# Layer 0's aggregate ahead of the last row block of layer 3's first product, its attention read with a stride

## The chip, the core and the metric

The kernel runs on one NeuronCore of a Trainium2 chip. The metric is the device time of one execution, in microseconds (us), of that core. All data are float32. The engines go by the profile's names: PE is TensorE's matmuls and PEld its weight loads, DVE is VectorE, ACT is ScalarE, POOL is GpSimd, SP is the queue that issues most plain DMAs.

## The reference, cut to what matters

Four graph layers follow each other on `x` of 128 samples x 128 nodes x 256 features, each with a residual and a layer norm. Layer 0 is an edge attention; the other three mix nodes with matrices made of `adj` and multiply by weights.

```python
# layer 0: 512 edges (src, dst), 4 heads of 64 features
Xq = (H @ W_lin.T).reshape(bt, n, h, dh);  Xv = (H @ W_val.T).reshape(bt, n, h, dh)
e = einsum('behd,hd->beh', leaky_relu(Xq[:, src] + Xq[:, dst], 0.2), a) + log(A0[src, dst] + 1e-8)
attn = segment_softmax(e, src)                     # over the edges of one source node
Y = segment_sum(attn[..., None] * Xv[:, dst], src) # the aggregate
x = layernorm(x + Y.reshape(bt, n, d) @ W_out.T)
# layer 1: x = layernorm(x + three products with adj * adj between them)
# layer 2: x = layernorm(x + three products with split adj)
# layer 3: h = relu(batchnorm((A_hat @ x) @ W1.T)); x = layernorm(x + batchnorm(h @ W2.T))
```

Layer 3's batch norms need statistics over all samples, so the kernel has two phases: the first runs layers 0 to 2 and layer 3's first product, the second the rest of layer 3.

## The kernel before

The first phase works on 32 quads of four samples. `iteration(k)` runs one step of a software pipeline over five quads at once: `a = k-1` is in layers 2 and 3, `c = k` in the second and third products of layer 1, `b = k+1` gets its layer 0 aggregate and the start of layer 1, `e = k+2` its attention weights and `g = k+3` its query and value products and the gather of its edges. The order of every engine's instructions is the order in which the code is written: each engine executes its own instructions in that order, and semaphores hold an instruction until what it reads is there.

The attention weights of a quad go through memory. `scatter` writes them by an indirect DMA (on POOL's queue) into a dense matrix `attd` in DRAM, at row target x 128 + source, with R = 16 numbers in a row, one for each of the 4 samples x 4 heads. A DMA on SP's queue then loads the matrix as the tile `ad`: 128 partitions (targets), and on each 128 sources x 16 numbers. So the 128 attention weights of one sample and head lie 16 floats, that is 64 bytes, apart.

`by_row` copies `ad` into `adc`, in which these 128 weights lie beside each other. A call handles one sample (4 heads, 512 floats on each partition), and four calls make a quad. In `iteration` they are lambdas placed between the products of `second`, after products 1, 3, 8 and 10, and run on ACT. In `iteration_0` they stand around `third(0, 2)`, in `start` ACT and DVE take two each.

`stage_a` uses `adc`. For each sample and each half of the features it issues two matmuls, one for each head: the values `xv` (128 targets x 64 features) are the weights, and the head's 128 attention columns are the moving operand. `tile_position=(0, h * DH)` puts the two heads into the two column halves of the array. Each program matmul of float32 stands in the profile as two weight loads and two matmuls, so a quad's 16 are 32 in the trace (tile `py`). ACT copies each half of the result from PSUM to `yt`, 16 matmuls (tile `po`) multiply it by `wo`, and DVE adds the result to `xr` and normalizes.

In `iteration` the order on PE around this is: `second(c)`, `stage_f(a)` (tile `pa`), `values(g, i)` (tile `pq`), the four row blocks `hidden(a, 0..3)` of layer 3's first product (tile `ph` of line 552), `stage_a(b)` (lines 288 and 297), the transposes of `attention(e)` (tile `pat`), and `third(c)` (tile `p` of line 462). ACT copies each row block to `z` (line 555), then makes the two `yt` copies (line 291). The softmax of quad `e` is advanced a step after each `values` and each `hidden`. SP's and POOL's queues carry the load of `ad`, the store of `z` and the gathers in the order of `values`, `hidden`, `gather`, `scatter`. PSUM tiles come from a ring of 8 banks, `xt`, `yt`, `mx` and the like from a ring of 6.

Of the kernel before, what the change touches and what calls it, by code (L numbers as in the profile page):

```python
# [8 lines left out]
F32 = mybir.dt.float32  # L9
# [15 lines left out]
def gnn_stack(ctx: ExitStack, tc: tile.TileContext, x, adj, w_qv_t, a, w_out_t, src, dst,  # L25
# [14 lines left out]
    nc = tc.nc  # L40
    B, N, D = x.shape
    H, DH = a.shape
    E = src.shape[0]
    P = 128
# [3 lines left out]
    QB = 4  # L48
    NQ = B // QB
    R = QB * H  # L50
# [3 lines left out]
    K3 = F3 // P  # L54
# [8 lines left out]
    def ps(name):  # L63
        return psum.tile([P, 512], F32, tag="ps", name=name)
# [21 lines left out]
    def batch_norm(stats, c, vecs, scale, shift, slot):  # L86

        b, gamma, beta = (vecs[:, i, c:c + 1] for i in range(3))
        t = bn_t[:, slot]
        nc.vector.bn_aggr(t[:, 0:2], stats[:, c].rearrange("p q s -> p (q s)"))  # L90
        nc.scalar.activation(t[:, 2:3], t[:, 1:2], AF.Sqrt, bias=eps)
        nc.vector.tensor_scalar(t[:, 3:4], t[:, 0:1], b, b, op0=ALU.add, op1=ALU.subtract)
        nc.vector.reciprocal(t[:, 2:3], t[:, 2:3])
        nc.vector.tensor_mul(scale[:, c:c + 1], gamma, t[:, 2:3])
        nc.vector.scalar_tensor_tensor(shift[:, c:c + 1], t[:, 3:4], scale[:, c:c + 1], beta,
                                       op0=ALU.mult, op1=ALU.subtract, reverse1=True)
# [25 lines left out]
    def layer_norm(pool, r):  # L122
        mv = norm_stats(pool, r)
        norm_apply(pool, r, mv, norm_root(pool, mv))


    with ExitStack() as phase:
# [5 lines left out]
        quads = [Quad() for _ in range(NQ)]  # L133
# [7 lines left out]
        wk = phase.enter_context(tc.tile_pool(name="wk", bufs=2))  # L141
# [24 lines left out]
        def temp(name):  # L166
            return wk.tile([P, 512], F32, tag="t", name=name, bufs=6)
# [98 lines left out]
            s.ad = wk.tile([P, N * R], F32, tag="ad", name=f"ad{k}", bufs=1)  # L266
            nc.sync.dma_start(s.ad, ad[:N * N, :].rearrange("(t s) r -> t (s r)", s=N))

        def by_row(k, j, copy=None):

            s = quads[k]
            if j == 0:
                s.adc = wk.tile([P, R, N], F32, tag="adc", name=f"adc{k}", bufs=1)
            (copy or nc.scalar.copy)(s.adc[:, j * H:(j + 1) * H, :],
                                     s.ad.rearrange("p (s r) -> p r s", r=R)[:, j * H:(j + 1) * H, :])

        def stage_a(k):

            s = quads[k]
            yts = []  # L280
            for j in range(0, QB, 2):
                py = ps("py").rearrange("p (b c n) -> p b c n", b=2, c=DC)
                for t in range(2):
                    for dc in range(DC):
                        for h in range(2):
                            r0 = (j + t) * H + dc * 2 + h
                            d0 = dc * P + h * DH
                            nc.tensor.matmul(py[h * DH:(h + 1) * DH, t, dc, :], s.xv[:, j + t, d0:d0 + DH], s.adc[:, r0, :],
                                             start=True, stop=True, tile_position=(0, h * DH))
                yt = temp("yt").rearrange("p (b c n) -> p b c n", b=2, c=DC)  # L290
                nc.scalar.copy(yt, py)
                yts.append(yt)
            for j in range(0, QB, 2):
                po = ps("po").rearrange("p (b d) -> p b d", d=D)
                for t in range(2):
                    for dc in range(DC):
                        nc.tensor.matmul(po[:, t, :], yts[j // 2][:, t, dc, :], wo[:, dc, :],
                                         start=(dc == 0), stop=(dc == DC - 1))
                xj = s.xr[:, j:j + 2, :]
                nc.vector.tensor_add(xj, xj, po)  # L300
                layer_norm(wk, xj)
# [244 lines left out]
        def hidden(k, c):  # L546
            s = quads[k]
            if c == 0:
                s.zt = zpool.tile([P, K3, QB * N], F32, tag="z", name="z", bufs=1)
            ph = ps("ph3")  # L550
            for dc in range(DC):
                nc.tensor.matmul(ph, l3w1[:, dc, c * P:(c + 1) * P], s.ag[dc],  # L552
                                 start=(dc == 0), stop=(dc == DC - 1))
            if k < NQ - 1:
                nc.scalar.copy(s.zt[:, c, :], ph)
            nc.vector.bn_stats(st1[:, c, k, :], ph)
            if k == NQ - 1:
                kept["z"] = s.zt
                batch_norm(st1, c, bn1, sc1, sh1, c)
                nc.scalar.activation(s.zt[:, c, :], ph, AF.Relu, bias=sh1[:, c:c + 1], scale=sc1[:, c:c + 1])  # L560
            elif c == K3 - 1:
                nc.sync.dma_start(z_dram[k], s.zt.rearrange("p c n -> p (c n)"))
# [21 lines left out]
        def iteration(k):  # L584
            a, c, b, e, g = k - 1, k, k + 1, k + 2, k + 3
            has_c, has_b, has_e, has_g = c < NQ, b < NQ, e < NQ, g < NQ
            if has_b and b > 2:
                quads[b].xr = load_x(b)
            if a > 0:
                stage_e(a, c if has_c else None)  # L590
            elif has_c:
                late_sums(c)
            if has_c:
                between = {i: [] for i in range(14)}
                if has_e:
                    for c_, i in enumerate((0, 2, 7)):
                        between[i].append(lambda c_=c_: score(e, c_))
                if has_b:
                    for j, i in enumerate((1, 3, 8, 10)):
                        between[i].append(lambda j=j: by_row(b, j))  # L600
                if has_g:
                    between[11].append(lambda: values_in(g, quads[g].xg))
                second(c, between)
                if has_e:
                    score(e, NE - 1)
            if has_g and g + 1 < NQ:
                quads[g + 1].xg = load_x(g + 1, "xg", 1, ws)
            stage_f(a)
            steps = softmax_parts(e) if has_e else iter(())
            for i in range(QB):  # L610
                if has_g:
                    values(g, i)
                if i > 1:
                    next(steps, None)
            for i in range(K3):
                hidden(a, i)
                next(steps, None)
            if has_g:
                gather(g)
            if has_b:  # L620
                stage_a(b)
            if has_e:
                attention(e)
                scatter(e)
            if has_c:
                third(c, 0)
                if has_b:
                    third(c, 2)
                    third_mix(c, 0)
                    mix1(b, 0)  # L630
                    third_norm(c, 0)
                else:
                    third(c, 2, lambda: third_mix(c, 0))
                    third_norm(c, 0)
                third_mix(c, 2)
            if has_b:
                mix1(b, 2)
                first(b, 0)
            if has_c:
                third_norm(c, 2)  # L640
            if has_b:
                firsts(b)
# [7 lines left out]
        def iteration_0():  # L650

            late_sums(0)
            between = {i: [] for i in range(14)}
            between[1] = [lambda: attention(1), lambda: scatter(1)]
            for c, i in enumerate((2, 5, 7)):
                between[i].append(lambda c=c: score(2, c))
            second(0, between)
            score(2, NE - 1)
            gather(3)
            third(0, 0)  # L660
            steps = softmax_parts(2)
            next(steps)
            for j in (0, 1):
                by_row(1, j)
            third(0, 2)
            next(steps)
            for j in (2, 3):
                by_row(1, j)
            third_mix(0, 0)
            third_norm(0, 0)  # L670
            third_mix(0, 2)
            third_norm(0, 2)
            stage_a(1)
            for _ in steps:
                pass
            attention(2)
            scatter(2)
            stage_e(0)
            mix1(1, 0)
            mix1(1, 2)  # L680
            first(1, 0)
            firsts(1)

        def start():
# [164 lines left out]
            gather(2)  # L849
            for c in range(NE - 1):  # L850
                score(1, c)
            for j in range(QB):
                by_row(0, j, nc.vector.tensor_copy if j % 2 else None)
            stage_a(0)
            for i in range(QB):
                values(3, i, nc.scalar.copy)
# [23 lines left out]
    with ExitStack() as phase:  # L880
        bufs = phase.enter_context(tc.tile_pool(name="bufs", bufs=1))
        cst = phase.enter_context(tc.tile_pool(name="cst3", bufs=1))
        keep = phase.enter_context(tc.tile_pool(name="keep", bufs=1))
        wk = phase.enter_context(tc.tile_pool(name="wk3", bufs=2))
# [294 lines left out]
```

## Time and profile before

| what | value |
|---|---|
| time, median of 3 runs | 3283.32 us (3282.48 to 3291.94) |
| the profiled execution's own time | 3313.41 us |
| its span, first to last instruction | 3311.7 us |
| mean granted TensorE clock in it | 0.991 |
| PE / PEld busy | 3204.4 us (97%) / 2388.9 us (72%) |
| DVE / ACT / POOL busy | 1923.6 us (58%) / 1188.8 us (36%) / 656.6 us (20%) |
| `py` matmuls, line 288 | 1024, in 32 groups of 32 |
| `adc` copies, line 274 | 126 on ACT, 2 on DVE |

All durations below come from the profiled execution, which took 0.9% longer than the median. A line "engine line out<-in ... xcount" of the timeline merges instructions of one form that follow each other; the number in brackets is the engine's idle time before it and what ended it. Matmuls overlap in the array, so the duration of one in a table (273 ns for a `py`) is longer than the time between the starts of two.

### The profile page before, as it was taken

The page shows a single profiled execution, that of the slowest core. Times are in us where ns is not written, and L with a number is a line of the kernel's source. Part 1 is how long each engine was busy: PE and PEld are TensorE (multiplying, and loading weights), DVE is VectorE, ACT ScalarE, POOL GpSimd, SP SyncE. Part 2 cuts the span into 40 slices and gives each one's busy share as a digit, 9 for nine tenths or more (in the row PEclk, how much of TensorE's full clock was granted, in tenths as well). Part 3 has the DMA queues.
Part 4 walks back from the last instruction along what each step waited for, and adds up shares of the span by engine and source line. Part 5 has one row for each costly group of instructions (what it writes and reads, how often), then busy time and mean ns, then how long its engine had stood idle before and what let it go on. Part 6 is the DMA issues. An engine that isn't in the chain of part 4 may idle for free. (4 is left out here: it accounts for less than half of the span.)

```text
span 3311.7 us, 38376 instructions
## 1 busy us (share of the span) xinstructions
PE 3204.4 (97%) x14804; PEld 2388.9 (72%) x14804; DVE 1923.6 (58%) x3702; ACT 1188.8 (36%) x2104; POOL 656.6 (20%) x541
## 2 busy tenths in 40 slices
PE   6899999999999999999999999999999999999997
PEld 3677777777777777777777777777777777784444
DVE  6655555555555655555555555555555555337888
ACT  2333333333333333333333333333333333325668
POOL 4211122222211111222222111112222220001135
PEclk7999999999999999999999999999999999999999
DMA  7612333333323223333333332233333331005557
GB/s 221 178 63 73 96 99 100 103 96 103 102 83 96 80 71 94 100 99 103 96 103 102 84 98 78 73 92 99 99 103 96 102 96 39 20 19 175 175 194 264
DMA packets 118742, 344.67 MB, mean 104 GB/s; under 512 B 15008, under 2 KB 51744, under 8 KB 110240
## 3 DMA queue, kind: packets, MB, share of 16 engines
q0 software_dynamic: 45552, 151.55, 18.3%
q1 hardware_dynamic: 70960, 188.71, 16.0%
q8 instruction: 117, 1.92, 0.2%
q10 hardware_dynamic: 2048, 1.97, 0.2%
q14 instruction: 65, 0.53, 0.1%
HBM read 256.20 MB, written 85.98 MB: 103 GB/s over the span
## 5 line engine op out<-in xcount | busy, mean ns | idle before, releaser
L208 POOL DMA_INDIRECT zs<-qd,src_idx x124 | 136.5, 1101 | 1668.1 <-DVE e L239 1563.3
L382 PE MATMUL ph<-m,w 128*128 128x256 f32 x2048 | 463.3, 379 | 0.0
L462 PE MATMUL p<-w,h 128*128 128x256 f32 x2048 | 450.6, 380 | 0.0
L462 PEld LDWEIGHTS p<-w,h 128*128 128x128 f32 x2048 | 386.6, 190 | 53.0 <-issue 1.0
L382 PEld LDWEIGHTS ph<-m,w 128*128 128x128 f32 x2048 | 386.7, 190 | 51.3
L382 PE MATMUL ph<-m,w_s 128*128 128x256 f32 x1536 | 352.4, 379 | 0.0
L510 PE MATMUL po<-l2w,ms 128*128 128x256 f32 x1536 | 348.1, 380 | 1.3 <-DVE ms L502 1.3
L382 PEld LDWEIGHTS ph<-m,w_s 128*128 128x128 f32 x1536 | 291.8, 190 | 39.7
L510 PEld LDWEIGHTS po<-l2w,ms 128*128 128x128 f32 x1536 | 284.9, 190 | 36.3 <-DVE ms L502 1.5
L475 DVE TENSOR_TENSOR xr<-xr,po 128x512 f32<-128x512 f32 x64 | 43.8, 684 | 350.1 <-PE po L473 350.0
L322 PE MATMUL ph<-w,mx 128*128 128x512 f32 x512 | 235.9, 593 | 0.9 <-ACT mx L311 0.9
L192 PE MATMUL pq<-wqv,xt 128*128 128x512 f32 x512 | 232.8, 599 | 0.2 <-ACT xt L180 0.2
L552 PE MATMUL ph<-ag,l3w 128*128 128x512 f32 x512 | 225.3, 593 | 0.8 <-ACT ag L541 0.8
L208 POOL DMA_INDIRECT zs<-qd,dst_idx x124 | 192.8, 1555 | 126.8 <-DMA zs<-qd,src_idx 106.5
L264 POOL DMA_INDIRECT attd<-at,att_idx x128 | 127.3, 995 | 420.4 <-DMA attd<-at,att_idx 281.6
L395 DVE TENSOR_TENSOR h<-ph,u 128x512 f32<-128x512 f32 x128 | 88.2, 689 | 179.2 <-PE ph L382 124.3
L552 PEld LDWEIGHTS ph<-ag,l3w 128*128 128x128 f32 x512 | 97.0, 190 | 122.0 <-issue 112.2
L111 ACT ACTIVATE ln_sd<-ln_mv,eps 128x2 f32<-128x2 f32 x192 | 56.4, 294 | 314.1 <-DVE ln_mv L106 313.8
L465 ACT COPY s<-p 128x512 f32<-128x512 f32 x64 | 37.5, 585 | 366.2 <-PE p L462 366.2
L342 PEld LDWEIGHTS pm<-wt_t,h 128*128 128x128 f32 x1024 | 131.8, 191 | 49.9 <-issue 38.8
L192 PEld LDWEIGHTS pq<-wqv,xt 128*128 128x128 f32 x512 | 93.7, 193 | 96.2 <-issue 88.0
L389 ACT COPY u<-ph 128x512 f32<-128x512 f32 x128 | 74.9, 585 | 245.4 <-PE ph L382 245.4
(226 smaller groups left out, 5019.9 us busy)
## 6 DMA issues: line engine op xcount, KB each, us to landing
ad<-attd SPq DMA_DIRECT2D x32, 1024.0 KB, 4.8
zd<-z SPq DMA_DIRECT2D x31, 1024.0 KB, 8.2
zl<-zd SPq DMA_DIRECT2D x62, 512.0 KB, 3.6
xr<-in_x_dram SPq DMA_DIRECT2D x32, 512.0 KB, 5.9
x3d<-xr SPq DMA_DIRECT2D x32, 512.0 KB, 2.6
x3l<-x3d SPq DMA_DIRECT2D x32, 512.0 KB, 4.6
out_dram<-x3l POOLq DMA_DIRECT2D x31, 512.0 KB
qd<-qt SPq DMA_DIRECT2D x30, 512.0 KB, 2.6
```

What stands on the lines that cost most here:

```text
L111: nc.scalar.activation(sd, mv[:, :, 1], AF.Sqrt, bias=eps)
L192: nc.tensor.matmul(pq, s.xts[i // 2][:, i % 2, c, :], wqv[:, c, :], start=(c == 0), stop=(c == DC - 1))
L208: nc.gpsimd.indirect_dma_start(out=s.z[c], out_offset=None, in_=s.qd, in_offset=bass.IndirectOffsetOnAxis(ap=idx[:, c:c + 1], axis=0), com ...
L264: nc.gpsimd.indirect_dma_start(out=ad, out_offset=bass.IndirectOffsetOnAxis(ap=att_idx[:, c:c + 1], axis=0), in_=s.at[:, c, :], in_offset= ...
L322: nc.tensor.matmul(ph, s.mx[i // 2 * 2][:, i % 2, dc, :], w1_sb[:, dc, :], start=(dc == 0), stop=(dc == DC - 1))
L342: nc.tensor.matmul(pm[:, c // 2, c % 2, :], s.h1[i][:, c * P:(c + 1) * P], wt_t, start=True, stop=True)
L382: nc.tensor.matmul(bank[g][:, i].rearrange("p b n -> p (b n)"), wa[:, c, f:f + P], s.m2[:, blk_b, c].rearrange("p b n -> p (b n)"), start= ...
L389: nc.scalar.copy(to[g], y[g])
L395: nc.vector.tensor_add(block(g, row, col), bank[g], kept_[g])
L462: nc.tensor.matmul(p3[:, t * D:(t + 1) * D], s.h2[f // 2][:, f % 2, j + t, :], w3_sb[:, f, :], start=(f == 0), stop=(f == K2 - 1))
L510: nc.tensor.matmul(po[:, i % 2, :], mss[i][:, t, dc, :], l2w[:, t, dc, :], start=(n3 == 0), stop=(n3 == 3 * DC - 1))
L552: nc.tensor.matmul(ph, l3w1[:, dc, c * P:(c + 1) * P], s.ag[dc], start=(dc == 0), stop=(dc == DC - 1))
```

## The change

Three things are edited. `by_row` and its calls are removed, and with them the tile `adc`. The `py` matmuls and the `yt` copies leave `stage_a` for a new function `aggregate`, and read `ad` itself through a view in which the 128 columns of a head are 16 floats apart. `aggregate` is called from new places: in `iteration` ahead of the last `hidden(a, K3 - 1)`, in `iteration_0` after `third(0, 2)` and ahead of `third_mix(0, 0)`, in `start` directly ahead of `stage_a(0)`, as before.

```diff
-        def by_row(k, j, copy=None):
-            s = quads[k]
-            if j == 0:
-                s.adc = wk.tile([P, R, N], F32, tag="adc", name=f"adc{k}", bufs=1)
-            (copy or nc.scalar.copy)(s.adc[:, j * H:(j + 1) * H, :],
-                                     s.ad.rearrange("p (s r) -> p r s", r=R)[:, j * H:(j + 1) * H, :])
-
-        def stage_a(k):
+        def aggregate(k):
             s = quads[k]
-            yts = []
+            s.yts = yts = []
+            ad = s.ad.rearrange("p (s r) -> p r s", r=R)
             for j in range(0, QB, 2):
                 py = ps("py").rearrange("p (b c n) -> p b c n", b=2, c=DC)
                 for t in range(2):
...
-                            nc.tensor.matmul(py[...], s.xv[:, j + t, d0:d0 + DH], s.adc[:, r0, :],
+                            nc.tensor.matmul(py[...], s.xv[:, j + t, d0:d0 + DH], ad[:, r0, :],
                                              start=True, stop=True, tile_position=(0, h * DH))
                 yt = temp("yt").rearrange("p (b c n) -> p b c n", b=2, c=DC)
                 nc.scalar.copy(yt, py)
                 yts.append(yt)
+
+        def stage_a(k):
+            s = quads[k]
+            yts = s.yts
             for j in range(0, QB, 2):
                 po = ps("po").rearrange("p (b d) -> p b d", d=D)
...
         # iteration
-                if has_b:
-                    for j, i in enumerate((1, 3, 8, 10)):
-                        between[i].append(lambda j=j: by_row(b, j))
...
             for i in range(K3):
+                if i == K3 - 1 and has_b:
+                    aggregate(b)
                 hidden(a, i)
                 next(steps, None)
...
         # iteration_0
-            for j in (0, 1):
-                by_row(1, j)
             third(0, 2)
             next(steps)
-            for j in (2, 3):
-                by_row(1, j)
+            aggregate(1)
             third_mix(0, 0)
...
         # start
-            for j in range(QB):
-                by_row(0, j, nc.vector.tensor_copy if j % 2 else None)
+            aggregate(0)
             stage_a(0)
```

More of the change, by code (lines that the diff above doesn't have):

```diff
@@ L287, in stage_a @@
                             d0 = dc * P + h * DH
-                            nc.tensor.matmul(py[h * DH:(h + 1) * DH, t, dc, :], s.xv[:, j + t, d0:d0 + DH], s.adc[:, r0, :],
+                            nc.tensor.matmul(py[h * DH:(h + 1) * DH, t, dc, :], s.xv[:, j + t, d0:d0 + DH], ad[:, r0, :],
                                              start=True, stop=True, tile_position=(0, h * DH))
```

## Prediction

> **What bounds the kernel now.** I read the page's busy shares first, then the timeline of one iteration, then PE's waits, then the rows by form. PE is busy in 97% of the span and in every slice but the first two and the last; DVE, ACT and POOL stand at 58%, 36% and 20%. So time is bought on PE, or where PE is kept waiting. PE's waits sum to under 100 us, and the largest lies where the change is made:
>
> ```profile
> engine line waited for: us in total, times, longest us
> PE po L297 <- ACT yt L291: 22.6, 27, 3.9
> ...
> PE py L288 <- ACT adc L274: 9.9, 1, 9.9
> ```
>
> The `po` matmuls wait for the copy that makes their operand out of `py`. The timeline of one iteration shows it:
>
> ```profile
> 1508.34 7.03 PE L552 MATMUL ph<-ag,l3w 128*128 128x512 f32 x16
> 1515.30 1.97 PE L288 MATMUL py<-adc,xv 128*64 128x128 f32 x32
> 1517.86 1.99 PE L297 MATMUL po<-wo,yt 128*128 128x256 f32 x8 [0.59 <-issue]
> 1520.08 1.99 PE L297 MATMUL po<-wo,yt 128*128 128x256 f32 x8 [0.22 <-ACT yt L291]
> 1522.00 0.42 PE L254 MATMUL pat<-ident,e 16*128 16x16 f32 x4
> ```
>
> From the first `py` to the first `pat` 6.70 us pass. The work in it is shorter: the `py` start in pairs 7 ns apart, a pair each 109 ns, so 16 pairs take 1.75 us; the 16 `po`, 0.2155 us apart, take 3.45 us. 1.5 us are waiting. A period of PE is 91.1 us (from one group of `py` to the next), and the waiting goes into it one for one: in the iteration at 423.3 us the second `yt` copy starts 2.1 us after the first `py` instead of 4.1, the stretch lasts 5.55 us, and that period is 90.2 us. The rows by form price the rest (duration and count, busy us, mean ns, idle before):
>
> ```profile
> L274 ACT COPY adc<-ad 128x512 f32<-128x512 f32 x126 | 132.7, 1080 | 8.1 <-DMA ad<-attd 8.1
> L291 ACT COPY yt<-py 128x512 f32<-128x512 f32 x64 | 37.3, 585 | 80.1 <-PE po L297 46.1 <-PE py L288 23.6 <-remote 9.9
> L382 PE MATMUL ph<-m,w 128*128 128x256 f32 x2048 | 463.3, 379 | 0.0
> ```
>
> Two copies of 128x512 floats on ACT: 585 ns where the source is contiguous, 1080 where it is read at a step of 64 bytes. And PE never waits inside `second` (line 382: 0.0), where the `adc` copies run.
>
> **What the Trainium skill says.** "SBUF — State Buffer", section "Door 1: The DMA port swizzle", has a note on lines of 16 bytes: it takes at least two hits in a line to absorb the access latency, so a step is free for 4 floats at most. "Advanced Engine Details and Errata", section "SBUF Cachelines", repeats it. Neither gives a price for PE. The trace agrees for ACT: 1080 - 585 = 495 ns over 512 elements are 0.97 ns more for an element. On DVE the two strided copies take 600 ns, 1.17 ns an element with all overhead, which shows no extra price at that rate. No PE matmul of any length reads with a step in this trace, so the price there is open. "TensorE: Matmul & The Clock Gate", section "The mechanism" of its Part 3, says that matmuls on different tiles of the array overlap, some 4 ns apart; the trace agrees with 7 ns. So two moving streams are read at once.
>
> **The change, part by part.**
>
> 1. The ACT copies go: 126 x 1.08 us, in an engine at 36% and beside `second`, where PE waits 0.0. Worth nothing in the 30 iterations. If ACT were behind there, it would show as idle of line 382.
>
> 2. The move past the last row block, 30 times. In the built program PE's order is `ph` 0 to 2, the 32 `py`, `ph` 3, `po`, `pat`; ACT's is `z`, `yt`, `yt`, `z`. No DMA is added, and SP's and POOL's orders are unchanged; the `z` store behind the last `z` copy comes up to 1.2 us later (two 0.585 us copies ahead of it), and its next reader is an iteration away. The new wait, `py` for the load of `ad` itself, costs nothing: before, the `adc` copies inside `second`, 20 to 40 us earlier, waited for it once only, in `start`. Behind the waiting `py` stands all of PE, so that cover matters, but it is long. What is saved: `ph` 3 takes 4 x 0.428 = 1.71 us, in which the first copy (0.585) is done. The second copy often starts only when the PE group behind its own ends; now that group is `ph` 3, so it would be done some 0.9 us into the first `po` half, 0.8 us before it is needed. Summed over the 30 stretches, the first `po` starts 8.6 us later than the 1.75 us of `py` allow, the second half 23.0 us later than the end of the first, and of the other 8.7 us (refill of the pipeline, `pat`) I give it 3.4. **-35 us**, bounds -31.6 and -40. The cover for the `pat` behind it is DVE's last scan (1515.64 to 1516.83 us in the iteration shown, `pat` at 1522.00): no new wait.
>
> 3. `start`: `ad` has landed at 77.1 us (end of ACT's 8.07 us wait); the first `py` start at 78.27 and, kept back by the four copies, end at 82.3. With no copy they run from 77.15 and take 1.75 us at the old pace, 3.5 at half. `po` starts 3.4 or 1.6 us earlier, and DVE's chain behind it (4.44 us idle for `po`, then norm, `score(1, 3)`, and PE's 10.1 us wait for `es`) follows. **-3.4 or -1.6 us.**
>
> 4. `iteration_0`: `py` now runs ahead of the two `third_mix` matmul groups, DVE's norm chain starts 1.75 us later (3.5 at half pace), but its 3.37 us wait for `po` goes. **-1.6 us, or 0.**
>
> 5. The strided read, the open cost. Below zero is excluded: the matmuls and loads are the same in number. *Free*, if one element of 4 bytes per 0.85 ns and stream (109 ns / 128) is slow enough, as DVE's 1.17 ns seem to be. *Doubled*, if each element costs a second access: +109 ns a pair, 16 pairs, 30 quads: **+52.5 us**. At ACT's surcharge, 128 x 0.97 = 124 ns a pair: +59.5 us. *Fourfold*, if besides the two streams no longer overlap: 3 x 52.5 = +157 us.
>
> I take doubled: ACT, at 585 / 512 = 1.14 ns an element the nearest in rate to a PE stream, pays for the step, and the skill's rule says that every reader does; DVE's two copies alone speak against it, and no contiguous DVE copy of SBUF stands beside them. Sum against the profiled execution: -35 - 1.6 + 52.5 = +16, of 3313.4, 0.5%. The median stands 0.9% below that execution, which leaves +16: 3283.3 + 16 = **3299 us**.
>
> **Rivals.**
>
> - *The step is free on PE, and only the gain is left* (36%). For it: DVE's two copies; 0.85 ns an element are two cycles of the 2.4 GHz that the TensorE page gives, so the array itself asks for a new element only every second cycle. Against it: ACT's row. -35 - 3.4 - 1.6 = -40: **3243 us**. It decides from a surcharge of under 40 / 52.5 = 76% of the doubling down.
> - *A part of the doubling* (10%): only one stream of a pair held up, or half the surcharge: -40 + 26 = -14, **3269 us**.
> - *Both streams are served in turn* (16%): one read port for two heads' columns, each element a line of its own. For it: two streams already ask for two elements per 0.85 ns. Against it: the pair runs at full pace now. +157 - 35 = +122: **3405 us**. PE would then hold `po` no longer, but be longer itself.
> - *The wait is replaced*: the second `yt` copy stays late by a whole group more and holds the second `po`; then the 23.0 us stay. I keep it inside the ranges: nothing shows a lateness of two groups.
> - That the order does not change is out: the built program has it.
>
> **How the numbers follow.** Doubled or ACT's surcharge, 38%: +9 to +28, that is 3292 to 3311. Free 36%: 3236 to 3250. Part 10%: 3255 to 3285. Fourfold 16%: left out. The range **3234 to 3313** holds 84%, less the edges. A measurement of this kernel tells about 0.3% (10 us) from no change. Faster by more: free, and most of the part, 0.43. Within: the rest of the part and the low end of doubled, 0.11. Slower: 0.46. The likeliest case alone has 3290 to 3312.
>
> **What would show it.** In the changed profile's timeline: `ph` x12, `py` x32, `ph` x4, `po` x16, `pat`. Step 5: the `py` group's length is 1.97 us if free, 3.6 to 4.1 if doubled, over 7 if fourfold, and a pair's spacing 109, 218 or 436 ns. Step 2: the wait of `po` for `yt` falls from 22.6 us to under 5, and the period of PE is 91.1 - 1.2 + the `py` surcharge (1.75 if doubled: 91.6; free: 89.9). Step 3: the first `py` within 0.3 us of the landing of `ad`. I am wrong if the period misses both, or if DVE or ACT get a row that PE waits for in the 30 iterations.

## The result, and the profile after

The changed kernel takes 3336.4 us (median of 4 runs, 3332.1 to 3340.8), the kernel before 3286.3 us beside it: a ratio of 1.0151, with a 95% interval of 1.0129 to 1.0173. It is 50 us slower; the forecast was 16 us slower, 3299 us. The kernel before has two kinds of sets of runs (a set is a series of runs made together on one chip), one at 3282 to 3293 us (this comparison and sets 1, 3 and 5 of the experiments) and one at 3311 to 3323 us (sets 2 and 4, and the profile that the forecast was made from).

The page of the changed kernel has PE busy longer, ACT 123 us less busy, and DVE nearly as it was:

```profile
PE 3252.0 (98%) x14804; PEld 2411.4 (72%) x14804; DVE 1916.9 (58%) x3700; ACT 1065.4 (32%) x1978; POOL 660.0 (20%) x541
```

PE's waits (total, times, longest) no longer hold the row of `po` for `yt`. Of the rows at the place of the change one is left, the first load of `ad` in `start`:

```profile
PE py L281 <- DMA ad<-attd: 7.0, 1, 7.0
```

The timeline of one iteration, PE alone:

```profile
785.80 3.69 PE L281 MATMUL py<-ad,xv 128*64 128x128 f32 x32
789.42 1.98 PE L550 MATMUL ph<-ag,l3w 128*128 128x512 f32 x4
791.24 3.62 PE L295 MATMUL po<-wo,yt 128*128 128x256 f32 x16
794.79 0.42 PE L254 MATMUL pat<-ident,e 16*128 16x16 f32 x4
```

The order is as built, with the last row block between `py` and `po`. No line has an idle time in brackets: PE runs through. But the 32 `py` take 3.69 us, where they took 1.97, and from their first to the row block behind them 3.62 us pass. The rows by form (count, busy us, mean ns, idle before) say the same, 399 ns a matmul where it was 280, and no wait in `second`:

```profile
L380 PE MATMUL ph<-m,w 128*128 128x256 f32 x2048 | 463.3, 379 | 0.0
...
L281 PE MATMUL py<-ad,xv 128*64 128x128 f32 x1024 | 119.4, 399 | 7.0 <-DMA ad<-attd 7.0
```

A period of PE (first `py` to first `py`) is 91.64 to 91.92 us in the inner iterations. The forecast said 91.6 for a doubled read. So the changed kernel does what the likeliest case said. What was wrong is the picture of the kernel before, as the first experiment shows.

### The profile page after: what moved, and what is told of

The parts are those of the page before. It is cut to its first block, busy times and chain, and to the rows that moved or that the text cites. A ratio compares the mean times of both kernels' runs of the same rounds, so it can differ in the third digit from the quotient of the medians.

```text
span 3330.4 us, 38305 instructions
## 1 busy us (share of the span) xinstructions
PE 3252.0 (98%) x14804; PEld 2411.4 (72%) x14804; DVE 1916.9 (58%) x3700; ACT 1065.4 (32%) x1978; POOL 660.0 (20%) x541
## 3 DMA queue, kind: packets, MB, share of 16 engines
q10 hardware_dynamic: 2048, 1.97, 0.2%
## 5 line engine op out<-in xcount | busy, mean ns | idle before, releaser
L550 PE MATMUL ph<-ag,l3w 128*128 128x512 f32 x512 | 233.3, 599 | 0.8 <-ACT ag L539 0.8
L554 DVE BATCH_NORM_STATS2 st<-ph 128x6 f32<-128x512 f32 x128 | 88.3, 690 | 148.8 <-ACT z L553 147.2
```

## The experiments

**Theories.** A stretch is PE's time from the first `py` of a quad to the first `pat`. P: the 1.5 us of waiting in each stretch of the first profile is not in the timed executions; there PE's period was already 89.9 us, the move saves nothing, and the doubled read is the whole loss. R: the wait is in every execution, and the read costs 85 us, more than a doubling.

### Set 1: the parts, each alone

*before_again*, no edit.

> The kernel before, unchanged. Theory P (the late second yt copy is a matter of the profiled execution: there it happens in 26 of 30 iterations, in a timed execution seldom): the profiled execution is 20 to 30 us longer than the timed median (3286), and its trace again shows most second yt copies about 4.1 us after the first py. Theory R (the wait is in every execution, and the strided read costs more than a doubling outside the profile): profiled and timed executions agree within 10 us, and the first profile was an outlier by chance.

Measured: 3288.9 us (3282.5 to 3292.0), its profiled execution 3283.8. The timeline of PE in one iteration of this profile, then ACT's:

```profile
1500.80 1.97 PE L288 MATMUL py<-adc,xv 128*64 128x128 f32 x32
1502.70 3.72 PE L297 MATMUL po<-wo,yt 128*128 128x256 f32 x16
1506.35 0.41 PE L254 MATMUL pat<-ident,e 16*128 16x16 f32 x4
```
```profile
1502.00 0.58 ACT L291 COPY yt<-py 128x512 f32<-128x512 f32 x1 [0.51 <-PE py L288]
1502.87 0.58 ACT L291 COPY yt<-py 128x512 f32<-128x512 f32 x1 [0.29 <-PE py L288]
```

The second `yt` copy starts 2.07 us after the first `py`, as soon as its group is done, the 16 `po` stand in one line, and `pat` follows the first `py` by 5.55 us instead of 6.7. All 30 stretches of this trace are like that, 27 of the 29 periods between them are 89.92 or 90.2 us, and PE's wait of `po` for `yt` is 3.9 us in one place (`iteration_0`) instead of 22.6 us in 27:

```profile
PE po L297 <- ACT yt L291: 3.9, 1, 3.9
```

So the wait is not in these executions. But profiling does not cause it either, as theory P had it: here profiled and timed executions agree.

*e1_move*: the copies and `adc` stay, `aggregate` goes where the change puts it.

```diff
             for i in range(K3):
+                if i == K3 - 1 and has_b:
+                    aggregate(b)              # reads s.adc
                 hidden(a, i)
...
```

> The move alone: the adc copies stay, aggregate goes ahead of the last row block. Theory P: little is left to gain in a timed execution, 30 times the 0.3 us of refill and what start and iteration_0 give: 3286 - 8 = 3278 us, between -3 and -15; its profiled execution no longer stands above its timed median, and is some 35 us shorter than the profiled execution before. Theory R: 31 to 40 us shorter in timed executions too, about 3250 us.

Measured: 3281.7 us, ratio 0.9988 (0.9981 to 0.9996), and 0.9996 (0.9987 to 1.0005) in set 5. The period stays 89.92 us: in the iterations the move saves nothing. The first `py` of the steady iterations starts at 236.9 us instead of 241.6 in *before_again* (240.6 in *before_3*); 1.7 us of that is the earlier place, 2.0 to 3.0 us are saved ahead of it. P's forecast, 3 to 15 us shorter, fits here, R's does not.

*e2_stride*: the copies go, `aggregate` is called by `stage_a` alone and so stays directly ahead of `po`.

```diff
         def stage_a(k):
+            aggregate(k)                      # reads s.ad with a step of 16 floats
             s = quads[k]
...
```

> The strided read alone: the adc copies go, aggregate stays in stage_a directly ahead of the po matmuls. Both theories: py takes 3.6 us for 32 matmuls, 1.87 us more in 30 iterations, +56 us on PE. Theory P: 3286 + 56 + 0 to 5 = 3342 to 3347 us timed, that is only 5 to 12 us above the change as a whole (3336). Theory R: the change as a whole is 50 us slower with 35 us gained by the move, so the read alone costs 85: about 3371 us.

Measured: 3329.9 us, ratio 1.0125 (1.0109 to 1.0140); 1.0144 (1.0127 to 1.0161) in set 3. The timeline of PE in one iteration:

```profile
512.16 3.68 PE L281 MATMUL py<-ad,xv 128*64 128x128 f32 x32
515.77 3.72 PE L296 MATMUL po<-wo,yt 128*128 128x256 f32 x16
519.42 0.42 PE L254 MATMUL pat<-ident,e 16*128 16x16 f32 x4
```

Periods are mostly 91.64 or 91.82 us. The read alone, 41 to 46 us, makes nearly the whole loss. R, with 3371 us, is out; P's 3342 to 3347 is too high too, by 12 us at its lower end and by 8 in sets 3 and 5.

*after_again*, no edit of the changed kernel.

> The change as a whole, again, beside its parts on one chip. Both theories: 50 us above before, about 3336 us, period of PE 91.65 us. Theory P: the profiled execution agrees with the timed median within 5 us, since no PE wait follows a py group here.

Measured: 3338.5 us, ratio 1.0150 (1.0136 to 1.0164). With the read strided the move brings nothing either: 2 to 9 us more than *e2_stride* in sets 1, 3 and 5. No trace shows a cause. The 9 us of set 1 may be the clock in part: three of the four *e2_stride* runs there had a granted clock of 0.992, the changed kernel's 0.989 to 0.991.

### Set 2: what a step costs

*step2* and *step4*: as *e1_move*, but ACT writes `adc` with the columns of a head 2 or 4 floats apart.

```diff
-                s.adc = wk.tile([P, R, N], F32, tag="adc", ...)
+                s.adc = wk.tile([P, R // w, N, w], F32, tag="adc", ...)   # w = 2, 4
...
-                                 s.xv[...], s.adc[:, r0, :],
+                                 s.xv[...], s.adc[:, r0 // w, :, r0 % w],
```

> The move with the adc copies kept (as in e1_move), but ACT writes adc so that a head's columns lie 2 floats, 8 bytes, apart: two hits in each 16-byte line. Theory line (one hit in a line costs a second access, two hits cost nothing): py keeps 109 ns a pair, 1.97 us a group, and the time is that of e1_move, about 3282 us. Theory element (a fetch brings 8 bytes, or only a step of 1 is free): doubled already, 218 ns a pair, about 3335 us.

> The same with the columns 4 floats, 16 bytes, apart: one hit in each line. Both theories: 218 ns a pair as with 16 floats, period 91.7 us, about 3335 us. If the price grew with the step instead, it would lie between step 2 and step 16.

*apart*: the change as a whole, the heads paired otherwise.

```diff
-                for t in range(2):
-                    for dc in range(DC):
-                        for h in range(2):
+                for dc in range(DC):
+                    for t, h in ((0, 0), (1, 1), (1, 0), (0, 1)):
```

> The change as a whole, the order of the py matmuls altered: the two that run side by side belong to different samples, so their columns lie in different 16-byte lines (floats 0 and 5 of the 16), not beside each other in one. Theory own (each of the two streams is held up by its own second access): no difference, 218 ns a pair, 3336 us. Theory shared (one port reads lines for both streams in turn, and the neighbouring floats of one line are served by one read): the pair would need twice the lines, up to 436 ns, up to 3336 + 105 = 3441 us.

*single*: the change, and `wt_t` of `mix1` and `mix2` read from a tile `[P, N, 16]` at `[:, :, 0]`.

> The change as a whole, and beside it the moving matrix of the first two node mixes of layer 1 (mix1 and mix2, 1536 matmuls of 128x128 on the whole array, one stream) is read from a copy with a step of 16 floats. Theory own: each of these pays for itself, 128 columns 218 instead of 109 ns, 1536 x 0.109 = +167 us, about 3503 us. Theory shared (only two streams together exceed what the port gives): a single stream stays at 109 ns, about 3336 us.

Measured: *step2* 3286.4 us, *step4* 3342.1, *apart* 3334.6, *single* 3492.4. The rows by form of *step2*, *step4* and *apart*:

```profile
L274 ACT COPY adc<-ad 128x512 f32<-128x512 f32 x126 | 76.5, 634 | 6.3 <-DMA ad<-attd 6.3
L288 PE MATMUL py<-adc,xv 128*64 128x128 f32 x1024 | 67.7, 283 | 9.4 <-ACT adc L274 7.8 <-DVE adc L274 1.6
```
```profile
L288 PE MATMUL py<-adc,xv 128*64 128x128 f32 x1024 | 123.5, 408 | 8.9 <-ACT adc L274 7.6 <-DVE adc L274 1.3
```
```profile
L280 PE MATMUL py<-ad,xv 128*64 128x128 f32 x1024 | 118.0, 396 | 6.9 <-DMA ad<-attd 6.9
```

At 8 bytes a matmul is nearly as long as contiguous (283 against 280 ns, pairs 114 ns apart against 109), at 16 bytes as long as at 64 (408 and 399; 228 and 218 ns). So the price does not grow with the step: it is absent where two elements lie in 16 bytes, there where one does, and it is a doubling. *apart* is no slower than the change, 218 ns a pair: that the two streams of a pair read neighbours in one line is no help, and theory *shared* falls. *single* settles it, by its row of `mix2` beside that of the changed kernel:

```profile
L341 PE MATMUL pm<-wt_w,h 128*128 128x128 f32 x1024 | 238.4, 393 | 0.0
```
```profile
L340 PE MATMUL pm<-wt_t,h 128*128 128x128 f32 x1024 | 133.8, 278 | 2.3 <-ACT h L323 2.2
```

One stream on the whole array pays as well: 218 ns from start to start instead of 112, in all 3492.4 - 3334.6 = 158 us over *apart* of the same set, for 1536 matmuls 0.103 us each. Each stream is held up by itself.

The kernel before took 3318.8 us in this set (3316.6 to 3321.6), 30 us more than in set 1, on the same chip some minutes later. *step2*, with the move and the copies kept, did not: 0.9906 of it (0.9889 to 0.9922). *apart*, which does what the change does, is 1.0047 (1.0030 to 1.0063). In this set the forecast difference of 16 us comes out with *apart* in the change's place (3334.6 - 3318.8), though the forecast time of 3299 us does not.

### Sets 3 to 5: the two kinds of set

*swap*: the kernel before with the heads of a pair exchanged.

```diff
-                        for h in range(2):
+                        for h in (1, 0):
```

> The kernel before once more. In one set of runs it took 3282 to 3293 us in every execution, in the next 3317 to 3322, and its first profile 3313. Theory set (in some sets of runs the signal of a py group reaches ACT late, whatever the kernel; it costs the kernel before 30 us because po follows py at once): this set is one of the two kinds; with the time near 3318 the profile has the second yt copy at about 4.1 us after the first py in most of the 30 stretches and a period of 91.05 us, with the time near 3285 it is at 2.07 us and the period 89.92. Theory chance (single executions fall into it): both kinds of time within this set.

> The kernel before with the two heads of a pair in the other order, so that the matmul which ends a py group and signals ACT lies in the array's lower column half (position 0) instead of the upper (64). Theory half (only a signal from the upper half can be late): about 3285 us in either kind of set. Theory pair (a signal after two overlapping matmuls can be late, whichever half): as the kernel before, 3318 in a late set, 3285 in another.

> The strided read alone once more. Theory set: its py groups take 3.6 us, and in the sets so far no signal after strided matmuls came late, so it takes 3330 us in either kind of set: 12 us above the kernel before in a late set, 41 above in another. If its signals can be late too, 3330 + 30 = 3360 in a late set.

> The change as a whole once more. Theory set: 3336 us in either kind of set, since the last row block lies between py and po; the ratio to the kernel before is 1.005 in a late set and 1.015 in another.

Measured in set 3, in this order: 3288.8, 3289.3, 3334.4 and 3336.2 us, the kind of set 1 throughout; *swap* could not tell anything.

> The kernel before once more, to meet a set of the late kind. Theory set: near 3318 us with the second yt copy at about 4.1 us after the first py in most stretches and a period of 91.05 us, or near 3285 us with that copy at 2.07 us and a period of 89.92.

> The order of the two heads exchanged. In a late set: theory half gives 3285 us, theory pair 3318. In another set both give 3285 and nothing follows.

Set 4 was of the other kind: *before_4* 3314.8 us (3311.2 to 3318.9), *swap_4* 3315.5. No execution of it came near 3290, so it is the set, not chance. The timeline of *before_4*, PE and then ACT:

```profile
1515.17 1.97 PE L288 MATMUL py<-adc,xv 128*64 128x128 f32 x32
1517.07 1.99 PE L297 MATMUL po<-wo,yt 128*128 128x256 f32 x8
1519.98 1.99 PE L297 MATMUL po<-wo,yt 128*128 128x256 f32 x8 [0.92 <-ACT yt L291]
```
```profile
1516.41 0.59 ACT L291 COPY yt<-py 128x512 f32<-128x512 f32 x1 [0.55 <-PE py L288]
1519.34 0.59 ACT L291 COPY yt<-py 128x512 f32<-128x512 f32 x1 [2.35 <-PE po L297]
```

By the profile's ends, which are modelled, the `py` end on PE as early as in set 1, but ACT learns of it 2 us later. The trace also has the times at which the semaphore that PE steps and ACT waits for moves. In *before_again*, *before_3*, *swap* and *e1_move* it moves 22 to 26 ns after the end of the last `py` in all 30 stretches. In the first profile, *before_4* and *swap_4* it moves 2.0 to 2.2 us after it in 26 of the 30; the first half of the `py` is late too, by 0.7 us or more, in 5 to 8 of these. Every other group of matmuls is signalled within 15 ns in *before_4*, except the `po` right behind (up to 0.2 us). So the lateness is on PE's side and not in ACT's queue; a late signal and a late true end of the matmuls cannot be told apart here. It is not shown to be bound to the end of the group behind either: where the first half is late too, as in the iteration of the first profile that the prediction shows, the second copy starts 0.3 to 0.4 us before the modelled end of the `po` group:

```profile
1519.44 0.58 ACT L291 COPY yt<-py 128x512 f32<-128x512 f32 x1 [1.63 <-remote]
```

That group runs from 1517.86 to 1519.85 us. In the other late stretches the copy starts 0.3 to 0.4 us after that end, and the profile names `po`, which the copy does not read, as the releaser.

The 4 stretches on time are the same ones in the first profile, *before_4*, *swap_4* and *step2*; 26 x 1.15 us = 30 us is the distance between the two kinds of set. *swap_4* has 26 late ones, so theory *half* falls; theory *pair* fits, but no run without overlapping pairs tests it. *step2*, in set 2, has the late copy as well, 3.8 us after the first `py`; there the last row block covers it, and no `po` waits. The expectation of *e2_stride_3* took strided groups to be on time in every set. In set 2 some are not: 6 of 30 second copies in *step4*, 3 in *apart* and 7 in *single* start 0.3 to 0.8 us late, and the row block covers these too.

> The move alone, to be met in a late set beside the kernel before. Theory set: about 3285 us in either kind of set, so 30 us below the kernel before in a late set (3315) and 3 to 7 us below it in another; in a late set its second yt copy starts late too, at about 3.8 us after the first py, behind the last row block, and no po waits for it.

> The strided read alone. In a late set: 3330 us if the signals of strided py groups come on time, 3360 if they come late as those of contiguous ones do. In another set 3330 and nothing follows.

> The change as a whole. Theory set: about 3335 us in either kind of set, 17 to 20 us above the kernel before in a late set (0.5 to 0.6%), 47 to 50 in another.

Set 5 was of the first kind again: 3282.7, 3334.5 and 3337.0 us, ratios 0.9996, 1.0144 and 1.0152. The move alone and the stride alone in a set of the late kind were therefore not seen; *step2* and *apart* stand for the move and for the change as a whole, the stride alone has no stand-in. What makes a set late stays open.

## Why the prediction was wrong, point by point

- **The step that failed is part 2 of the sum, "the move past the last row block": -35 us.** In the set in which the change was measured it is worth nothing in the iterations: the kernel before is at 3286 us there, and in the sets of that kind its period is 89.92 us with and without the move. Its premise, 1.5 us of waiting in each stretch, was read from a profiled execution that took 3313.4 us where the median was 3283.3. The prediction noted these 0.9% and scaled by them, as if they lay evenly over the span. They lay in that very wait: 26 stretches of 1.15 us are 30 us, the whole gap, so a gain was taken from a median that already lacked the wait. Against the profiled execution the sum holds, 3313.4 + 16 = 3329 us, where the changed kernel's profiled execution took 3332.1. Four stretches of that trace showed the ordinary course; the prediction used one of them (5.55 us, period 90.2) to show that the wait counts, and it was the better model of a timed run. Without part 2 the same sum is 52.5 - 1.6 = +51, 3334 us, against 3336.4 measured.
- The wait was real where it occurs: the run *step2* against the kernel before in set 2 is 32 us, the lower bound of part 2 being 31.6. The reason given for it, that the second copy starts when the PE group behind its own ends, is not what the iteration shown has: the copy starts at 1519.44 us, that group ends at 1519.85.
- **Part 5, the strided read: the mechanism and the size were right.** 218 ns a pair and 3.6 us a group were forecast for a doubling and measured. From the first to the last of the 30 steady groups the changed kernel takes 2647.0 to 2651.1 us in its four profiles and *before_again* 2597.3: 50 to 54 us more, where 29 doubled groups make 51. The free read (36% given) and the fourfold one are out: a group takes 3.69 us and not 1.97 or over 7, and *apart* and *single* show each stream paying for itself. "SBUF — State Buffer", section "Door 1: The DMA port swizzle", was the right guide in its need of two hits in a 16-byte line, as *step2* shows; its free step of 4 floats, which the prediction repeats, does not hold here, since at 4 floats (*step4*) the full price is due.
- ACT's row was the right neighbour. With two neighbouring floats to each 16 bytes (*step2*) its copies take 634 ns instead of 1080, so the step made them long, not the difference between PSUM and SBUF as a source. DVE's row was misread as free of a price: with two or four neighbours (*step2*, *step4*) one of its two copies takes 407 and 416 ns instead of 600, the other 739 and 610, so 600 ns was no sign of a free step.
- Parts 1, 3 and 4: no PE wait in `second`, as forecast. In the changed kernel's four profiles the first `py` of the steady iterations starts at 235.8 to 236.8 us, 3.8 to 5.8 us ahead of *before_3* and *before_again*. Less 1.7 us for the earlier place, `start` and `iteration_0` gave 2.1 to 4.1 us, where 1.6 were in the doubled case.
- The new wait of `py` for `ad` occurs once, in `start`, for 7.0 us, as forecast: before, ACT waited there.

## What to carry to other kernels

Ask first where the gap between a profiled execution and the timed median lies: if a step's gain is about as large as that gap, it may be the gap. A moving operand of float32 whose elements lay 16 or 64 bytes apart cost PE twice the stream time here; a copy on an engine with slack that brings two neighbours into 16 bytes was enough to avoid it. Work put between a group of matmuls and the readers of its copy was cheap insurance against a late signal: it cost nothing in the ordinary sets (*e1_move*) and was worth 32 us in a late one (*step2*).

## What the runs showed of the hardware that was not expected

- The signal that ends a group of overlapping column-half matmuls can reach ACT some 2 us late: in 26 of 30 groups of both profiled executions of the kernel before at 3313 to 3316 us, and in none of the two at 3283 us. It went with the set of runs (two of five), not with the chip (sets 1 and 2 shared one), nor with the column half (*swap_4*). Which 4 groups are on time went with their place in the program.
- The doubling comes at once: 109 ns a pair at 4 bytes, 114 at 8, 228 at 16, 218 at 64; and it holds for one stream alone (112 to 218 ns).
